# The first scan round's responses and state additions ahead of the placing of the choices, and the last block of the first expert layer ahead of the moments

## The chip, the cores and the metric

One NeuronCore of a Trainium2 chip runs the whole kernel in one launch. The metric is the device time in microseconds (us); lower is better. Three runs of the kernel before gave 1929.3, 1924.45 and 1923.44 us, so its median is 1924.45 us. The profile is of a fourth execution that took 1926.27 us.

## The reference, cut to what matters

The input is 8 sequences of 1024 tokens with 256 features. Two layers follow each other, each adding an attention-like part and a mixture of experts (MoE) to its input. Only the first layer is touched here:

```python
xn = _layernorm(x)
x = x + _L0_attn_ref(xn, ...) + _L0_ffn_ref(xn, ...)

# _L0_attn_ref: a linear state space scan of 16 states per feature, along the sequence
def step(h, x_t):
    h = jnp.einsum('dnm,bdm->bdn', A, h) + Bm[None] * x_t[..., None]
    y_t = jnp.einsum('dn,bdn->bd', Cm, h) + Dm * x_t
    return (h, y_t)
_, y = jax.lax.scan(step, h0, jnp.swapaxes(x, 0, 1))
y = gelu(_layernorm(y, ln_w, ln_b)) @ W_out.T + b_out      # then x + y

# _L0_ffn_ref: 8 experts, 2 chosen for each token, and a shared expert
topk_idx = jax.lax.top_k(masked, TOPK)[1]
y = jnp.einsum('tei,eih->teh', _silu(g) * u, w_down)       # the chosen experts' rows are summed by weight
```

The second layer normalizes this sum, takes one matrix product as its attention, and has an MoE of 8 experts with a fixed capacity.

## The kernel before, in words

The tokens lie as 64 tiles of 128 (`NT`), 8 tiles (`TPB`) to a sequence. The tile `y` holds them all, 128 x 64 x 256 in fp32; it is overwritten stage by stage. The line numbers are those of the kernel before.

**Stage 1, to about 205 us.** Each pair of tiles is normalized, turned, put through the router (L606) and the shared expert (L265, L280, L617). Every second sequence `route0` (L489) picks two experts for 16 tiles; the fourth `route0` ends this stage. Its steps are small VectorE instructions (L493 to L531, and L204 to L214 in the helper `pick_two`).

**The places (L662 to L723).** All choices of all tokens are counted, and each gets a place in a list sorted by expert, in blocks of 256 rows. Two matmuls count (L672, L676), ScalarE brings the counts from PSUM (L673, L677), and VectorE does the rest: L680 sums along the tokens, L684 to L697 find where each expert's blocks begin, L698 to L713 give each choice its place, L717 to L723 name the expert of each of the 71 blocks.

**The scan in 8 rounds.** The recurrence is worked out with matrix powers. A round `bt` takes 4 groups of 8 features. `krylov(bt)` (L292) makes the powers: `begin` (L301 to L314), then 7 levels k = 1, 2, 4 to 64; each level has for each of the 4 groups two matmuls into a PSUM tile `pk` (L324), then a VectorE copy (L331) and a ScalarE copy (L335, at the last level L333) out of it, on which the next level's matmuls of that group depend. There are two `pk` buffers. `rest(bt)` (L343) returns 16 steps that use the powers: `responses` (L348: matmuls L359, VectorE L368 and L369, and the DMA L372 of the responses to a DRAM scratch); four `adds` (L377: matmul L381, ScalarE copy L383, matmul L386, VectorE L390 of 0.6 us and L391 of 1.0 us); seven `chunk` (L398: matmuls L409, VectorE L413; the first is a copy, L402); four `outputs` (L417: the DMA L422 that loads the responses again, matmuls L433 and L438, and a copy of the round's features into `y`, L448 or L450).

**What is done between the steps.** The loop at L883 gives out, after each of a round's 16 steps, one step of `krylov(bt + 1)`, and a share of other work: in rounds 0 and 1 the `finds` (L730: VectorE L738, L741 and L745, ScalarE L749, matmul L751), which turn the places into lists of rows; in rounds 2 to 7 the 71 blocks of the first MoE. `block(n)` fetches the rows of block n + 1 (`bring`, L783: DMA L788 and gathers L791), finishes block n - 1 (`narrow`, L805: matmul L280, VectorE L810, scatter L813 into the DRAM tensor `yr`) and begins block n (`widen`, L801: L251, L255, L265, L270, L272, L273). The last block, number 70, is thus given out after the last step of the last round, and its own `narrow` follows it.

**The moments.** `first_moments` (L867) measures two sequences of the scan's finished output (16 pairs of L179 and L180 on VectorE), makes scales of them (L184 on ScalarE, L185 and L186 on VectorE) and normalizes the first sequence (8 times L191 on ScalarE). It is called after the last `outputs` and ahead of the last share of blocks.

**Stage 3, from about 782 us.** SyncE loads `base` and rows of `yr` (L955, L963), VectorE adds them (L976); meanwhile `flipped` (L923) turns and activates the normalized scan output (L932 on TensorE, L933 on ScalarE), `project` (L1003) multiplies by `W_out` (L1011) and adds (L1018); then moments again, and the second layer. From about 1000 us on the second MoE fills TensorE (L1415, L1433).

**What sets the order.** Each engine runs its own queue in order. The order in the queue is that of the source only roughly: a scheduler in the framework moves an instruction ahead of others where it expects it to be ready. In the kernel before it already draws the responses and additions of round 0 in among the instructions of the places, and the finds behind all levels of `krylov(1)`.

## Time and profile before

| what | value |
|---|---|
| median of three runs | 1924.45 us |
| the profiled execution, its time | 1926.27 us |
| its span in the trace | 1924.6 us (1.7 us lie around it) |
| mean granted TensorE clock | 0.969 |
| ScalarE, VectorE, GpSimd busy | 716.6 us (37%), 705.7 us (37%), 656.1 us (34%) |
| chain that ended last | TensorE 52% of the span, VectorE 3%, DMA 1%, ScalarE 1% |
| its largest lines | L1415 23%, L1433 23% (the second MoE), L1011 2% |
| first MoE's scatter, L813 | 142 times, 996 ns each |
| VectorE L179 (a tile's moments) | 128 times, median 397 ns |

How to read it: the trace gives the start of each instruction, its length, and, for a stretch in which the engine stood idle, what ended the wait. In the timeline a line has the start, the length, the engine, the line of the source with its operation, and in brackets the idle time before it with what ended it. PE is TensorE's matmuls, PEld its weight loads, DVE VectorE, ACT ScalarE, POOL GpSimd, SP SyncE; an engine's name with a q (SPq) is its queue, which issues DMAs. The granted clock is the share of TensorE's full clock that it was allowed. An fp32 matmul stands as two passes (x2).

### The profile page before, as it was taken

How to read it: one execution, taken by the hardware profiler on the slowest of the kernel's cores; microseconds unless marked ns; L12 is line 12 of the kernel's file. 1: busy time of each engine (PE TensorE's matmuls, PEld its weight loads, DVE VectorE, ACT ScalarE, POOL GpSimd, SP SyncE). 2: the span in 40 equal slices, each digit the busy share in tenths (PEclk: the TensorE clock that was granted, in tenths of full speed). 3: DMA queues.
4: the chain of work that ended last, by engine and by line, in shares of the span. 5: the costliest groups of instructions: out<-in, count | busy, mean ns of one | idle time of the engine just before them, and what ended most of it. 6: DMA issues, size and time to landing. Idle time of an engine off the chain costs nothing.

```text
span 1924.6 us, 24183 instructions
## 1 busy us (share of the span) xinstructions
PE 1790.2 (93%) x8619; PEld 1360.6 (71%) x8619; DVE 705.7 (37%) x2121; ACT 716.6 (37%) x1627; POOL 656.1 (34%) x668
## 2 busy tenths in 40 slices
PE   6987789999999999689959999999999999999996
PEld 5876667888888877579737667667666766766764
DVE  5854688444554444787751001101110110100110
ACT  6973354333333321679922222222222222222221
POOL 0000001666756766111023434343333333333322
PEclk9988899999999999889969999999999999999998
DMA  9565222565656666899533455443223232332211
GB/s 254 143 180 158 74 61 84 150 180 161 185 176 173 177 192 167 259 287 246 140 104 59 83 99 83 96 67 83 40 47 72 40 81 35 64 61 34 40 17 22
DMA packets 218520, 224.77 MB, mean 117 GB/s; under 512 B 50776, under 2 KB 190880, under 8 KB 218272
## 3 DMA queue, kind: packets, MB, share of 16 engines
q0 software_dynamic: 56928, 90.29, 23.7%
q1 hardware_dynamic: 158784, 130.54, 23.6%
q10 hardware_dynamic: 2688, 2.40, 0.4%
q8 instruction: 68, 1.11, 0.2%
q14 instruction: 52, 0.43, 0.1%
HBM read 136.87 MB, written 89.46 MB: 118 GB/s over the span
## 4 chain that ended last, share of the span: by engine, by line
PE 52%; DVE 3%; DMA 1%; ACT 1%; issue 1%; POOL 0%; POOLq 0%; SPq 0%; DVEq 0%; ACTq 0%
PE phe L1415 23%; PE poe L1433 23%; PE pd L1011 2%; PE px L1398 1%; PE pt L932 1%; PE pd L1076 1%; DMA xs<-yr 1%; DMA out_dram<-yo,invi 1%; DVE hl L1160 0%; DVE hh L1165 0%; ACT y L191 0%; PE pi L1175 0%; DVE st L179 0%; PE pt L1057 0%; DVE hb L976 0%
## 5 line engine op out<-in xcount | busy, mean ns | idle before, releaser
L1433 PE MATMUL poe<-w2t,hT 128*128 128x256 f32 x2048 | 447.3, 379 | 0.0
L1415 PE MATMUL phe<-xTe,w1t 128*128 128x512 f32 x1024 | 446.2, 594 | 0.6 <-DVE xTe L1399 0.6
L1433 PEld LDWEIGHTS poe<-w2t,hT 128*128 128x128 f32 x2048 | 386.7, 190 | 51.7 <-issue 0.5
L1415 PEld LDWEIGHTS phe<-xTe,w1t 128*128 128x128 f32 x1024 | 195.0, 191 | 233.1 <-issue 229.9
L1445 POOL DMA_INDIRECT out_dram<-yo,invi x128 | 201.8, 1577 | 446.0 <-DMA out_dram<-yo,invi 226.0
L1422 ACT ACTIVATE hT<-phe,b1T 128x512 f32<-128x512 f32 x256 | 176.0, 687 | 247.3 <-PE phe L1415 242.9
L1444 ACT ACTIVATE yo<-yo,gr 128x256 f32<-128x256 f32 x128 | 58.0, 500 | 441.4 <-DVE yo L1440 441.4
L1440 DVE TENSOR_TENSOR yo<-poe,b2t 128x512 f32<-128x512 f32 x64 | 44.3, 692 | 406.6 <-PE poe L1433 406.6
L1384 POOL DMA_INDIRECT xg<-xd,invi x128 | 124.6, 974 | 192.0 <-PE px L1398 86.2
L1399 DVE COPY xTe<-px 128x512 f32<-128x512 f32 x64 | 41.2, 686 | 382.6 <-PE px L1398 382.6
L813 POOL DMA_INDIRECT yr<-yo,goes x142 | 141.4, 996 | 65.3 <-DVE yo L810 27.8
L791 POOL DMA_INDIRECT xb<-xnd,choice x142 | 141.0, 993 | 46.9 <-issue 32.6
L324 PE MATMUL pk<-kr 128*128 128x129 f32 (+7 forms) x896 | 140.9, 296 | 9.4 <-ACT kr L335 8.6
L324 PEld LDWEIGHTS pk<-kr 128*128 128x128 f32 x896 | 124.7, 196 | 24.6 <-ACT kr L335 14.2
L265 PE MATMUL pgu<-xT,wb 128*128 128x256 f32 x568 | 138.8, 387 | 0.8 <-ACT xT L255 0.7
L786 POOL COPY wb<-wrow 1x1 int32<-1x1 int32 x71 | 12.8, 180 | 368.3 <-PE pgu L751 320.2
L265 PEld LDWEIGHTS pgu<-xT,wb 128*128 128x128 f32 x568 | 105.8, 192 | 26.8 <-ACT xT L255 12.6
L335 ACT COPY kr<-pk 128x256 f32<-128x256 f32 x192 | 69.6, 373 | 86.7 <-DVE kr L331 84.7
L270 ACT ACTIVATE sg<-pgu 128x256 f32<-128x256 f32 x87 | 33.4, 384 | 170.2 <-PE pgu L265 170.1
L272 DVE TENSOR_TENSOR hh<-pgu,sg 128x256 f32<-128x256 f32 x87 | 36.9, 424 | 127.3 <-ACT sg L270 127.1
L280 PE MATMUL pd<-wb,hh 128*128 128x256 f32 x284 | 77.1, 394 | 5.4 <-DVE hh L273 5.4
L810 DVE SCALAR_TENSOR_TENSOR yo<-pd,xb,bhalf 128x256 f32<-128x256 f32 x142 | 62.2, 479 | 49.0 <-PE pd L280 44.5
(323 smaller groups left out, 2349.6 us busy)
## 6 DMA issues: line engine op xcount, KB each, us to landing
wb<-wpk SPq DMA_DIRECT2D x71, 384.0 KB, 3.4
xnd<-xr SPq DMA_DIRECT2D x32, 512.0 KB, 8.5
hk<-kscr SPq DMA_DIRECT2D x32, 512.0 KB, 4.5
hb<-yr POOLq DMA_DIRECT2D x10, 1024.0 KB, 14.4
base<-y SPq DMA_DIRECT2D x8, 1024.0 KB, 4.4
hb<-base SPq DMA_DIRECT2D x8, 1024.0 KB, 10.2
out_dram<-y SPq DMA_DIRECT2D x8, 1024.0 KB, 14.2
xd<-xs SPq DMA_DIRECT2D x8, 1024.0 KB, 12.7
```

Source lines behind the costliest of these rows:

```text
L265: nc.tensor.matmul(pgu[:, j, :], lhsT=gu[:, j, c, :], rhs=xT[:, c, :], start=(c == 0), stop=(c == DC - 1),)
L280: nc.tensor.matmul(pd[:, q, :], lhsT=hh[:, q * P : (q + 1) * P], rhs=wb[:, 2 * DC * I : WW], start=True, stop=True,)
L324: nc.tensor.matmul(pk[:, j, :n], lhsT=t[:, 1 - j, P:], rhs=t[:, j, P - k : P - k + n], start=True, stop=True,)
L335: nc.scalar.copy(t[:, :, P:], pk[:, :, k : k + P])
L791: nc.gpsimd.indirect_dma_start(out=xb[:, q, : D + 1], out_offset=None, in_=xnd[:, :], in_offset=bass.IndirectOffsetOnAxis(ap=choice[:, 2 * ...
L810: nc.vector.scalar_tensor_tensor(yo[:, q, :], pd[:, q, :], xb[:, q, D : D + 1], bhalf, ALU.mult, ALU.add)
L813: nc.gpsimd.indirect_dma_start(out=next(yr_own)[:, :], out_offset=bass.IndirectOffsetOnAxis(ap=goes[:, 2 * n + q : 2 * n + q + 1], axis=0) ...
L1384: nc.gpsimd.indirect_dma_start(out=xg[:, q, :], out_offset=None, in_=xd[:, :], in_offset=bass.IndirectOffsetOnAxis(ap=invi[:, q0 + q : q0 ...
L1415: nc.tensor.matmul(ph, lhsT=w1t[:, c, h * P : (h + 1) * P], rhs=xT[:, c], start=(c == 0), stop=(c == DC - 1),)
L1422: nc.scalar.activation(hT[:, h], ph, AF.Relu, bias=b1T[:, e * HC + h : e * HC + h + 1])
L1433: nc.tensor.matmul(po[:, r, :], lhsT=hT[:, h, q + r, :], rhs=w2t[:, h, :], start=(h == 0), stop=(h == HC - 1),)
L1445: nc.gpsimd.indirect_dma_start(out=of[:, :], out_offset=bass.IndirectOffsetOnAxis(ap=invi[:, q0 + r : q0 + r + 1], axis=0), in_=yo[:, r, : ...
```

## The change

The change has two parts.

First, `rest` no longer takes the pool `toep` as an argument; it looks it up when `outputs` runs. So the steps of round 0 can be made before that pool exists, and their first five, `responses` and the four `adds`, are called right after the last `route0`, ahead of the source lines of the places. In the loop, round 0 skips these five; what is given out between the steps (powers of round 1, finds) is not changed.

Second, `first_moments` is called after the loop, so behind the last share of blocks, and its scales are made for each of the two sequences by themselves: two calls of L184, L185 and L186 on 8 columns in place of one on 16.

```diff
-        def rest(bt, toep):
+        pools = {}
+
+        def rest(bt):
...
-                hk = toep.tile([P, CH, P], F32, name="hk")
+                hk = pools["toep"].tile([P, CH, P], F32, name="hk")
...
-                hm = toep.tile([P, CH, NT], F32, name="hm")
+                hm = pools["toep"].tile([P, CH, NT], F32, name="hm")
...
                             route0(2 * TPB, slice((b - 1) * TPB, (b + 1) * TPB))
 
 
+            round0 = rest(0)
+            begun = 1 + GB
+            for step in round0[:begun]:
+                step()
+
+
             full = [P, NT, E]
...
         with tc.tile_pool(name="eb", bufs=3) as eb_, tc.tile_pool(name="toep", bufs=2) as toep:
+            pools["toep"] = toep
...
             def first_moments():
 
+
                 for b in range(2):
-                    moments(mo, first_mv[:, b], y[:, b * TPB : (b + 1) * TPB, :], TPB)
-                scales(first_mv, first_rstd, first_off)
-                ys = y[:, :TPB, :]
-                normalize_act(ys, ys, first_rstd[:, 0], first_off[:, 0], TPB)
+                    ys = y[:, b * TPB : (b + 1) * TPB, :]
+                    moments(mo, first_mv[:, b], ys, TPB)
+                    scales(first_mv[:, b], first_rstd[:, b], first_off[:, b])
+                    if b == 0:
+                        normalize_act(ys, ys, first_rstd[:, b], first_off[:, b], TPB)
...
             for bt in range(NBT):
-                steps = rest(bt, toep)
+                steps = rest(bt) if bt else round0
...
                 for s, step in enumerate(steps):
-                    step()
+                    if bt or s >= begun:
+                        step()
                     if s < len(ahead):
                         ahead[s]()
-                    if bt == NBT - 1 and s == len(steps) - 1:
-                        first_moments()
                     for f in part(s):
                         f()
+            first_moments()
```

Built, the two kernels have the same instructions but for one more L184, L185 and L186 each. The orders of SyncE's and GpSimd's queues are the same. The other three queues differ in two places only: from the end of the last `route0` to level 4 of `krylov(1)`, and from the second-last block's L810 to the first instructions of stage 3.

## The prediction

> **What bounds the kernel now.** I read the page first, its busy shares and slices. TensorE is busy 93% of the span, so what counts is where it is not.

> ```profile
> PE   6987789999999999689959999999999999999996
> ...
> PEclk9988899999999999889969999999999999999998
> ```

> A slice is 48.1 us. The fifth (192 to 241 us) and the seventeenth to nineteenth (770 to 914 us) have low digits, and the two edits lie there. Next, windows of 6 us and TensorE's timeline for the first place:

> ```profile
> 218.00:224.00 6.00, 0.04 (x2) 0.03 (x1) 6.00 (x15) 0.37 (x1) 0.00 (x0) 0.91 0.00 0
> 224.00:230.00 6.00, 4.05 (x16) 3.60 (x16) 3.26 (x16) 1.39 (x4) 0.00 (x0) 0.50 0.39 108
> 230.00:236.00 6.00, 5.72 (x29) 4.95 (x29) 1.28 (x7) 2.52 (x7) 0.00 (x0) 0.73 0.28 71
> ```

> ```profile
> 216.99 1.02 PE L386 MATMUL pm<-xc,vT 128*128 128x448 f32 x2 [0.18 <-ACT vT L383]
> 223.97 1.25 PE L324 MATMUL pk<-kr 128*128 128x132 f32 x4 [5.96 <-ACT kr L335]
> 227.17 15.42 PE L324 MATMUL pk<-kr 128*128 128x132 f32 x72 [1.95 <-ACT kr L335]
> 245.64 0.49 PE L751 MATMUL pgu<-wb,xb 128*128 128x284 bf16 x2 [3.05 <-ACT wb L749]
> ```

> In a window row the busy times are of PE, PEld, DVE, ACT and POOL, then comes the clock. From 212 to 224 us VectorE is full; TensorE stands still for 5.96 us, and its clock falls to 0.50 until about 233. From 227 us krylov(1) runs alone: matmuls, L331, L335, in a circle. The first find (L738) starts at 243.00, behind the last L331 in VectorE's queue.

> For the second place, the timeline from 764 to 782 us:

> ```profile
> 766.52 0.75 DVE L179 BATCH_NORM_STATS2 st<-y 128x6 f32<-128x256 f32 x2 [1.05 <-ACT y L450]
> ...
> 769.99 0.38 ACT L270 ACTIVATE sg<-pgu 128x256 f32<-128x256 f32 x1 [2.08 <-PE pgu L265]
> ...
> 772.76 0.46 DVE L810 SCALAR_TENSOR_TENSOR yo<-pd,xb,bhalf 128x256 f32<-128x256 f32 x1
> ...
> 773.59 0.42 DVE L272 TENSOR_TENSOR hh<-pgu,sg 128x256 f32<-128x256 f32 x1
> ...
> 774.71 2.08 PE L280 MATMUL pd<-wb,hh 128*128 128x256 f32 x4 [4.76 <-DVE hh L273]
> ...
> 777.09 0.86 DVE L810 SCALAR_TENSOR_TENSOR yo<-pd,xb,bhalf 128x256 f32<-128x256 f32 x2
> ...
> 781.86 0.38 SPq L955 DMA_DIRECT2D hb<-base  x1
> ```

> ```profile
> SPq L955 <- DMA yr<-yo,goes: 24.6, 1, 24.6
> ```

> The last line is from the waits (total, times, longest). L280 of block 69 was through at 766.79, yet L810 comes at 772.76: 16 pairs of L179 and L180, at 0.39 us each, stand before it. Block 70's L272 was ready at 770.37 and comes at 773.59. SyncE's L955, which opens stage 3, waits for the last scatter: the end of the last L810 sets it, 4.77 us after that starts (777.09 to 781.86).

> **Part one, the early steps.** The built VectorE queue holds the same instructions between the last pick and level 4; only their order changes. I walked through the new order with start distances of the timeline: a 128x512 step 0.60 us, L390 0.54, L391 0.88, L697 0.94, a 0.29 us step 0.33 if the next needs it and 0.20 if not, small ones 0.10.

> - L368 goes ahead of L511 at about 202.1 us. Its matmuls L359 (4 in 1.06 us) stand behind L280, which starts at 199.95, and end by 201.7: no wait. The first L390 waits some 0.3 us for L381, L383 and L386, and L617 0.1 us, as its L280 is now behind that L386. In exchange the 0.76 us that L617 waits now goes.
> - The four pairs L390, L391 (4 x 1.42 = 5.7 us) then fill the gaps of the pick. L520, which gives the counts' matmuls their input, comes at 212.0 instead of 207.76, L684 at 216.9 instead of 212.87. Behind it the pairs are missing, so the places catch up: L697 at 220.7 (218.92), the last L713 at 225.7 (226.31). The VectorE work of the stretch is the same, so its end stays within a microsecond.
> - In the place of the pairs stand L331 copies. Now only two of level 4's four are done by 226.7, the others come at 228.46 and 229.34, and level 8 begins at 230.45. Then all four are done by 226.5, limited at the end by the two pk buffers (matmuls 0.6, L331 0.2, L335 0.37 us), and level 8 begins at 227.1.
> - TensorE's longest gap becomes 1.8 us (215.6 to 217.4), not 5.96. At full clock four copies take 3.0 us (levels 16 and 32: 233.94 to 236.99), at half clock 3.5 (level 8: 230.45 to 233.94). At full clock L738 comes at 227.1 + 12.55 - 0.5 = 239.15: **3.85 us** earlier. At half clock each of level 4's last copies waits 0.9 us for the next, level 8 begins at 228.6, L738 comes at 241.15: 1.85 us. Below, nothing: if my walk is too short by 2 us; above, 4.5.

> I take 3.5, near the full clock, as a gap of 3.18 us (780.87 to 784.04) left it at 1.00. [...]

> Queues passed: L372 stays behind the last L535 in SyncE's queue, so it leaves at about 216 instead of 214.39; L422 waits for L713 as now (226.56), and its matmul L438 comes at 268.7, so nothing is late. The four L383 (0.27 us) go ahead of L313 on ScalarE, which stands idle 6.61 us in this stretch. GpSimd has nothing here. The finds and blocks behind keep their order, so they all start earlier by the same.

> **Part two, the moments.** In the new VectorE queue one L179 stands before block 69's L810, which starts at 766.9 (its L280 is through at 766.79) and ends at 767.8. Eleven halves of pairs follow, to 770.2; L272 starts at 770.4, as soon as L270 (769.99 + 0.38) is through; L273 at 771.2, L280 from 771.7 to 772.75 at the full clock's 1.03 us (TensorE idle 1.75 us, not 4.76). L810 starts at 772.8 in place of 777.09, and L955 4.77 later, at 777.6: **4.2 us** earlier. At half clock L280 takes 2.08 and it is 3.2.

> What is late next? ScalarE: L191 starts at 774.3 (now 775.76), 8 of them take 4.0, the second L184 0.31, so L933's table load starts at 778.6 (781.91) and L933 at 779.9 (783.21): 3.3 us earlier. Its L1011 begins at 781.7, but L1018 needs L976 first (790.71), which waits for DMAs issued behind L955. The DMA share is 0.9 to 1.1 from 783 to 812, all of it issued after L955, so it moves by 4.2 as a whole, and L976, L1018, the moments and L1029 (802.05) with it. The second L191s come wholly behind L933 (8, not 6: 1.0 us more); ScalarE waits 7.70 us before L1029, which covers it. The added L184, L185, L186 (0.31, 0.24, 0.16) lie in these waits. From 812 us on the order is the same, and the chain is mostly TensorE's; I take the shift whole to the end.

> **Sum.** -3.5 - 4.2 = -7.7. From the profiled execution's 1926.27 (1924.6 and 1.7 around it) this gives 1918.6; from the median, 1.8 lower, 1916.7. I say 1917.5.

> **Rivals.**
> 1. *The clock stays at half through level 8.* 1.85 + 4.2 = 6.1: 1919.1. For it: from 215.6 to 224.4 TensorE works only some 3 of 8.8 us, and at 247 the clock fell after 1 of 4.8. Against: the gaps there were longer (3.05).
> 2. *Only the moments count*, as VectorE ends the places about 3 us later than in my walk: 4.2, or 1921.0. For it: the walk rests on 0.1 us distances, some 80 of them.
> 3. *Only the early steps count*: stage 3 opens at 777.6, but L933 or the loads are held by something not seen before. 3.5: 1921.7. Against: L955 waits for the same scatters in both built queues, and 7 us lie between L1011 and L1018.
> 4. *Slower: the copies hold VectorE.* Ten L331 now stand among the places. If each waits for a matmul at half clock, 1.5 us as the longest such wait now, that is 15 us: 1917.5 + 15 = 1932.5. It decides against the change from 0.8 us each. For it: now each L331 in the place stretch finds its matmul long done. Against: at most three of the ten come less than 0.6 us after the copy that frees their buffer.
> 5. *No change*, the built orders being no measure of time: 1925.

> **How the numbers follow.** 0.3%, or 5.8 us, is about what a measurement of this kernel can tell from none: the bound is 1918.7. Forecast 0.55, rivals one 0.17, two 0.10, three 0.08, four 0.05, five 0.05. The range: 4.5 + 4.8 (no wait at all before the last L810) off the lowest run, 1923.44, gives 1914; only the half-clock 3.2, off the mean of median and profiled time, gives 1922. It leaves out rivals four and five and edges. Faster: 0.50 of the forecast, 0.08 of rival one, 0.04 of two and three, 0.62; slower 0.05; the rest, 0.33, within.

> **What would show it.** TensorE's clock at 224 to 230 us near 1 and no gap over 2 us from 215: else rival one. L331 of level 8 near 227 and L738 near 239: else two. Relative to L450's end: last L810 6.3 us after it (now 10.6), L955 11.1 (now 15.4), L976 from 20 (now 24.2): else three. Waits of L331 among the places over 0.8 us: four. I would be wrong wholly if stage 3's first loads waited for the moments instead of the last scatter.

## The result, and the profile after

| | before | after |
|---|---|---|
| median, runs | 1923.51 us, 22 runs (1920.95 to 1930.35) | 1918.81 us, 22 runs (1912.27 to 1926.0) |
| ratio, 95% interval | | 0.9975 [0.9965, 0.9984] |
| profiled execution, span | 1926.27, 1924.6 us | 1920.38, 1918.7 us |

The change makes the kernel faster by 0.25%, 4.7 us. The forecast was 1917.5 us (1914 to 1922) and its sum 7.7 off. So the time lies in the range, while the sum was too large by 3.0 us.

In the changed kernel the line numbers are higher: of those that count here L672, L676 (the counts' matmuls) are L680, L684; L520 is L522, L698 is L706, L713 is L721, L390 and L391 are L392 and L393, L386 is L388, L738 is L747, L450 is L452, L810 is L819, L955 is L966, L976 is L987, L1415 is L1426. L265 to L335 keep theirs.

The busy slices of the page of after, for TensorE and its clock:

```profile
PE   6987799999999998889869999999999999999996
...
PEclk9988899999999999889979999999999999999998
```

TensorE's fifth digit is 7 as before and the clock's is 8 as before: the first place is not visibly better. At the second place the seventeenth digit has gone from 6 to 8. Next the windows of after from 206 to 230 us (busy time of PE, PEld, DVE, ACT and POOL, then the clock), and TensorE's timeline there:

```profile
206.00:212.00 6.00, 4.53 (x12) 2.50 (x12) 4.40 (x18) 1.92 (x4) 0.00 (x0) 0.72 0.15 1
212.00:218.00 6.00, 3.75 (x16) 3.03 (x16) 5.91 (x24) 1.39 (x4) 0.00 (x0) 0.71 0.17 7
218.00:224.00 6.00, 4.53 (x18) 4.08 (x19) 4.31 (x23) 1.77 (x5) 0.00 (x0) 0.50 0.02 4
224.00:230.00 6.00, 5.42 (x32) 4.31 (x31) 1.51 (x9) 2.98 (x8) 0.00 (x0) 0.94 0.63 175
```

```profile
202.79 1.02 PE L388 MATMUL pm<-xc,vT 128*128 128x448 f32 x2
207.29 1.65 PE L680 MATMUL pm<-hot,before 128*128 128x512 f32 x2 [3.48 <-DVE kr L331]
208.73 1.91 PE L684 MATMUL pm<-hot,ones 128*128 128x512 f32 x2
...
213.81 3.75 PE L324 MATMUL pk<-kr 128*128 128x130 f32 x16 [1.99 <-ACT kr L335]
218.76 1.25 PE L324 MATMUL pk<-kr 128*128 128x132 f32 x4 [1.21 <-ACT kr L335]
```

The gap of 5.96 us is gone, but a new one of 3.48 us stands ahead of the counts' matmuls. The clock falls behind it: those matmuls take 1.65 and 1.91 us, where 1.10 and 1.02 were needed before, and from 216 to 224 us the clock is at 0.50. VectorE, whose queue has L706 next, waits for them, which it didn't before (L698). In the timelines of before:

```profile
208.20 1.10 PE L672 MATMUL pm<-hot,before 128*128 128x512 f32 x2
209.13 1.02 PE L676 MATMUL pm<-hot,ones 128*128 128x512 f32 x2
...
210.22 0.68 DVE L698 TENSOR_TENSOR hot<-hot,first 128x512 f32<-128x512 f32 x1
```

And in VectorE's of after, where it waits later for level 4's matmuls too:

```profile
210.68 0.69 DVE L706 TENSOR_TENSOR hot<-hot,first 128x512 f32<-128x512 f32 x1 [1.43 <-PE pm L684]
...
222.00 0.17 DVE L331 COPY kr<-pk 128x8 f32<-128x8 f32 x1 [0.47 <-PE pk L324]
...
222.88 0.17 DVE L331 COPY kr<-pk 128x8 f32<-128x8 f32 x1 [0.51 <-PE pk L324]
```

The second place, after's timeline from 759 to 772 us, and the wait ahead of stage 3:

```profile
759.36 0.59 ACT L452 COPY y<-py 128x512 f32<-128x512 f32 x1 [1.35 <-PE py L440]
...
759.98 0.43 DVE L179 BATCH_NORM_STATS2 st<-y 128x6 f32<-128x256 f32 x1 [1.05 <-ACT y L452]
...
760.32 0.86 DVE L819 SCALAR_TENSOR_TENSOR yo<-pd,xb,bhalf 128x256 f32<-128x256 f32 x2
...
763.86 0.42 DVE L272 TENSOR_TENSOR hh<-pgu,sg 128x256 f32<-128x256 f32 x1 [0.30 <-ACT sg L270]
...
765.06 1.13 PE L280 MATMUL pd<-wb,hh 128*128 128x256 f32 x4 [1.65 <-DVE hh L273]
...
766.23 0.88 DVE L819 SCALAR_TENSOR_TENSOR yo<-pd,xb,bhalf 128x256 f32<-128x256 f32 x2
...
771.38 0.38 SPq L966 DMA_DIRECT2D hb<-base  x1
```

```profile
SPq L966 <- DMA yr<-yo,goes: 20.7, 1, 20.7
```

One L179 stands ahead of block 69's L819 and L272 waits for ScalarE alone. L966 still waits for the last scatter, and comes 12.0 us behind the start of the last L452, in place of 15.9.

**Where the time went.** The two spans differ by 5.9 us, but that this is near the medians' 4.7 is chance: in 13 profiles the last scores of stage 1 (L653, in changed kernels L655 or L656, on ScalarE), which no edit touches, start anywhere from 188.5 to 198.4 us. So I cut each profile at events that both kernels have, in us. "scores to find" goes from the start of that last ScalarE instruction to the first find (L738, L747), "find to y" to the start of the last copy into `y` (L450, L452), "y to base" to SyncE's first base load (L955, L966), "base to MoE" to the second MoE's first matmul (L1415, L1426), and "MoE to end" to the end of the span.

| profile | scores to find | find to y | y to base | base to MoE | MoE to end |
|---|---|---|---|---|---|
| before | 44.7 | 522.9 | 15.9 | 216.5 | 926.2 |
| after | 43.5 | 522.8 | 12.0 | 219.8 | 927.5 |
| e1 early steps only | 43.9 | 521.0 | 15.9 | 217.3 | 927.3 |
| e2 moments only | 44.7 | 520.9 | 12.7 | 219.3 | 927.6 |
| e3 after, gap filled | 42.6 | 523.1 | 12.0 | 217.5 | 927.1 |
| e4 counts first | 41.3 | 520.8 | 12.0 | 217.2 | 927.1 |
| e5 before again | 44.7 | 597.5 | 15.9 | 218.7 | 927.3 |
| e6 after again | 43.5 | 604.3 | 12.3 | 217.8 | 926.9 |
| e7 scales undivided | 43.7 | 598.6 | 12.4 | 216.1 | 926.9 |
| e8 counts first, gap filled | 40.9 | 596.5 | 12.1 | 217.4 | 927.1 |
| e9 after, timed | 43.8 | 586.9 | 12.3 | 219.5 | 927.4 |
| e10 counts first, timed | 41.4 | 581.5 | 12.2 | 218.1 | 927.3 |
| e11 counts first, gap filled, timed | 41.0 | 578.4 | 12.1 | 217.9 | 927.2 |

Columns one and three hardly vary from execution to execution: a kernel's repeats agree within 0.5 us. They hold the effect: -1.2 and -3.9, together 5.1 us, against 4.7 measured. The chips of e5 to e8 and of e9 to e11 are other ones, with a longer stretch from find to y; there only comparisons within a chip count.

### The profile page after: what moved, and what is told of

Same layout as the page of the kernel before. It is cut to its first block, busy times and chain, and to the rows that moved or that the text cites. A ratio compares the mean times of both kernels' runs of the same rounds, so it can differ in the third digit from the quotient of the medians.

```text
span 1918.7 us, 24190 instructions
## 1 busy us (share of the span) xinstructions
PE 1794.2 (94%) x8619; PEld 1363.5 (71%) x8619; DVE 706.1 (37%) x2123; ACT 716.4 (37%) x1628; POOL 655.9 (34%) x668
## 4 chain that ended last, share of the span: by engine, by line
PE 58%; DVE 4%; DMA 2%; ACT 2%; issue 1%; POOL 0%; POOLq 0%; SPq 0%; DVEq 0%; ACTq 0%
PE phe L1426 23%; PE poe L1444 23%; PE pgu L265 2%; PE pd L1022 2%; PE px L1409 1%; PE pd L1087 1%; PE pt L943 1%; PE pd L280 1%; DMA xb<-xnd,choice 1%; PE py L440 1%; PE pk L324 1%; DMA out_dram<-yo,invi 1%; DVE st L179 1%; ACT hh L1184 0%; DVE hb L987 0%
## 5 line engine op out<-in xcount | busy, mean ns | idle before, releaser
L1426 PE MATMUL phe<-xTe,w1t 128*128 128x512 f32 x1024 | 447.2, 595 | 0.6 <-DVE xTe L1410 0.6
L1426 PEld LDWEIGHTS phe<-xTe,w1t 128*128 128x128 f32 x1024 | 195.4, 191 | 233.8 <-issue 230.6
L1410 DVE COPY xTe<-px 128x512 f32<-128x512 f32 x64 | 41.3, 687 | 383.7 <-PE px L1409 383.7
L822 POOL DMA_INDIRECT yr<-yo,goes x142 | 141.4, 996 | 60.1 <-DVE yo L819 31.8
L324 PE MATMUL pk<-kr 128*128 128x129 f32 (+7 forms) x896 | 140.8, 295 | 5.5 <-ACT kr L335 4.9
L265 PE MATMUL pgu<-xT,wb 128*128 128x256 f32 x568 | 140.3, 391 | 1.0 <-ACT xT L255 0.7
L324 PEld LDWEIGHTS pk<-kr 128*128 128x128 f32 x896 | 124.5, 196 | 21.2 <-ACT kr L335 10.1
L265 PEld LDWEIGHTS pgu<-xT,wb 128*128 128x128 f32 x568 | 106.4, 193 | 27.7 <-ACT xT L255 13.3
L335 ACT COPY kr<-pk 128x256 f32<-128x256 f32 x192 | 69.7, 373 | 85.2 <-DVE kr L331 82.6
L270 ACT ACTIVATE sg<-pgu 128x256 f32<-128x256 f32 x87 | 33.4, 384 | 171.1 <-PE pgu L265 171.0
L272 DVE TENSOR_TENSOR hh<-pgu,sg 128x256 f32<-128x256 f32 x87 | 36.9, 424 | 129.5 <-ACT sg L270 129.3
L819 DVE SCALAR_TENSOR_TENSOR yo<-pd,xb,bhalf 128x256 f32<-128x256 f32 x142 | 62.1, 479 | 48.2 <-PE pd L280 47.7
L280 PE MATMUL pd<-wb,hh 128*128 128x256 f32 x284 | 76.0, 389 | 2.1 <-DVE hh L273 2.0
## 6 DMA issues: line engine op xcount, KB each, us to landing
out_dram<-y SPq DMA_DIRECT2D x8, 1024.0 KB, 11.4
```

The costliest lines, as they stand in the source:

```text
L265: nc.tensor.matmul(pgu[:, j, :], lhsT=gu[:, j, c, :], rhs=xT[:, c, :], start=(c == 0), stop=(c == DC - 1),)
L280: nc.tensor.matmul(pd[:, q, :], lhsT=hh[:, q * P : (q + 1) * P], rhs=wb[:, 2 * DC * I : WW], start=True, stop=True,)
L324: nc.tensor.matmul(pk[:, j, :n], lhsT=t[:, 1 - j, P:], rhs=t[:, j, P - k : P - k + n], start=True, stop=True,)
L335: nc.scalar.copy(t[:, :, P:], pk[:, :, k : k + P])
L819: nc.vector.scalar_tensor_tensor(yo[:, q, :], pd[:, q, :], xb[:, q, D : D + 1], bhalf, ALU.mult, ALU.add)
L822: nc.gpsimd.indirect_dma_start(out=next(yr_own)[:, :], out_offset=bass.IndirectOffsetOnAxis(ap=goes[:, 2 * n + q : 2 * n + q + 1], axis=0) ...
```

## The experiments

**The two parts alone.** My theory at this point: the moments give 4 us, the early steps 1, since the new gap costs them the clock. The first kernel has only the early steps:

```diff
-            first_moments()
+                    if bt == NBT - 1 and s == len(steps) - 1:
+                        first_moments()
```

(with `first_moments` as before), the second has the early steps taken out:

```diff
-            for step in round0[:begun]:
-                step()
```

(and round 0 made in the loop again). Expected of them, on record:

> Only the early steps (responses and additions ahead of the places); the moments stay where they were before. Theory: the early steps are worth little, since TensorE now stands 3.5 us ahead of the counts' matmuls and runs them and krylov's next levels at half clock; last scores to first find 43.5 us (44.7 before, 43.5 after), first L450 on ScalarE to the first base load 16.0 as before, time about 1922.3 (1.2 off). Rival one, the sum on record: the early steps are worth 3.5 us and it is the gain of the moments that is lost: 1920.0, scores to find 41. Rival two, they are worth nothing but noise: 44.7 and 1923.5.

> Only the moments behind the last block; the early steps stay behind the places as before. Theory: the shorter way from the last outputs to the first base load (12.0 in place of 16.0 us) is kept to the end, and the 4 us by which the stretch from the roots to the mixture's first matmul was longer in the profile of after are that execution's own: time 1919.5, roots to the mixture about 196 to 198. Rival, the gain is given back in the third stage by the order itself: same 12.0 us, but roots to the mixture about 200, time 1922.5 to 1923.5.

Measured: early steps only 1922.87 us against 1923.46 of before on that chip, ratio 0.9989 [0.9976, 1.0002]; moments only 1921.16, 0.9982 [0.9967, 0.9997]. The times alone tell the parts from nothing barely or not at all; the stages tell them well. With the early steps alone, scores to find is 43.9 and y to base 15.9; with the moments alone 44.7 and 12.7. Each part moves its own stretch and leaves the other's as it was. The sum on record for part one (41) is out. The second expectation also asked for the time from the roots (the first L1029 of the next moments) to the second MoE's first matmul: 198.1 us with the moments alone, against 196.3 in before's and 200.3 in after's first profile. That is just above the theory's 196 to 198 and not the rival's 200; the time of the run lies between the two forecasts. In the profile of the early steps alone the same gap stands, with the same price:

```profile
211.88 1.87 PE L680 MATMUL pm<-hot,before 128*128 128x512 f32 x2 [3.50 <-DVE kr L331]
213.55 1.91 PE L684 MATMUL pm<-hot,ones 128*128 128x512 f32 x2
```

**The gap filled.** Into after's gap I put three products that nobody reads:

```diff
                 nc.scalar.copy(vT, pv[:, :P])
+                m["vT"] = vT
...
             for step in round0[:begun]:
                 step()
+            warm = ps_d.tile([P, 2, D], F32, name="pd").rearrange("p q d -> p (q d)")
+            for _ in range(3):
+                nc.tensor.matmul(
+                    warm[:, : CH * NS1], lhsT=m["vT"],
+                    rhs=xcols[:, (GB - 1) * CH : GB * CH, :NS1], start=True, stop=True,
+                )
```

> After, with three more products of the last addition's operands (L388's, 128x448, about 0.5 us each at full clock) into a bank that nobody reads, between the last addition's product and the counts' matmuls, so that TensorE stands still for under 2 us there. Theory, the clock is what part one lacks: the granted clock stays near 1 from 206 to 212 us and mostly to 224, the counts' matmuls take 0.9 us each in place of 1.65 and 1.91, last scores to first find falls from 43.5 to about 41.5 to 42.5, time 1917.5. Rival, VectorE's order is what it lacks: the clock rises but scores to find stays within 0.4 of 43.5, time 1918.8 as after. Third, 1.5 us of work are too little for the clock: it falls as in after, and the run tells nothing on the two.

Measured: 1919.56 us, 0.9981 [0.997, 0.9991]; scores to find 42.6. Its TensorE timeline, the first copy of level 8 in VectorE's, and windows:

```profile
204.00 2.42 PE L671 MATMUL pd<-xc,vT 128*128 128x448 f32 x6
207.65 1.10 PE L687 MATMUL pm<-hot,before 128*128 128x512 f32 x2 [1.24 <-DVE kr L331]
208.59 1.02 PE L691 MATMUL pm<-hot,ones 128*128 128x512 f32 x2
...
223.84 0.17 DVE L331 COPY kr<-pk 128x16 f32<-128x16 f32 x1 [0.74 <-PE pk L324]
```

```profile
210.00:214.00 4.00, 1.66 (x13) 1.27 (x11) 3.91 (x22) 1.10 (x4) 0.00 (x0) 1.00 0.54 12
214.00:218.00 4.00, 1.71 (x10) 1.33 (x11) 4.00 (x10) 0.89 (x3) 0.00 (x0) 1.00 0.00 0
218.00:222.00 4.00, 2.76 (x13) 2.42 (x13) 3.02 (x17) 1.02 (x3) 0.00 (x0) 0.56 0.03 6
222.00:226.00 4.00, 4.00 (x19) 3.67 (x19) 0.91 (x7) 1.57 (x5) 0.00 (x0) 0.59 0.70 186
```

(The products are 0.8 us each, not 0.5 as I wrote: the three stand as six passes, which took 2.42 us.) The clock stays at 1.00 until 218 us, the counts' matmuls take 1.10 and 1.02 again, and the wait of 1.43 us for them is gone from VectorE's timeline. The last place (L713 of before, L728 here) starts 28.6 us behind the last scores instead of 30.0. So the clock theory holds, for 0.9 of the 2.6 us by which part one stayed under its full-clock figure (3.85 less 1.2). The rest is not the clock at the counts. The clock still falls at 218 (0.56 from 218 to 222 us), while levels 2 and 4 give TensorE little to do (1.71 of 4 us from 214), and level 8 begins 30.4 us behind the scores; that these levels come so late because the counts stand behind the pairs is what the next kernel tries. The time of the run is no lower than after's, and 1917.5 was forecast; a microsecond can't be told from none here, only the stage shows it.

**The counts first.** If the pairs ought not to delay the step that feeds the counts, the steps can be given behind the counts' matmuls and still ahead of the places:

```diff
             round0 = rest(0)
             begun = 1 + GB
-            for step in round0[:begun]:
-                step()
...
             nc.scalar.copy(tot, pc.rearrange("p (i e) -> p e i", e=E))
+            for step in round0[:begun]:
+                step()
             cum = spare(4, [P, E, NT])
```

> After, but the responses and additions are given behind the two counts' matmuls and their copies, and still ahead of the places. In the built VectorE queue the step that feeds the counts (L520 of before) then comes ahead of the four pairs again, and the pairs stand among the first places. Theory: TensorE gets its counts' matmuls some 10 us after the last scores as before (14.2 in after), at full clock, and no gap over 3 us follows, so scores to find falls below after's 43.5, to about 42.5, time 1918. Rival: the pairs delay the copies of levels two and four as they did before, scores to find 44.7, time 1919.8, that is only the moments' gain.

Measured: 1917.52 us in 6 runs, 0.9967 [0.9952, 0.9983]; scores to find 41.3, better than the theory's 42.5. Its "no gap over 3 us" was wrong: TensorE stands still for 5.62 us later, and level 8 starts at half clock (0.50 from 224 to 228 us). Its timeline:

```profile
208.31 1.10 PE L678 MATMUL pm<-hot,before 128*128 128x512 f32 x2
...
217.57 0.84 PE L324 MATMUL pk<-kr 128*128 128x132 f32 x6
224.03 1.25 PE L324 MATMUL pk<-kr 128*128 128x132 f32 x4 [5.62 <-ACT kr L335]
```

What it gains beyond the filled gap's 42.6 is VectorE's order. In its timeline the first of level 4's copies (128x8) has gone ahead of the last two pairs, and the last starts at 225.5, 27.1 us behind the last scores (after: 30.9). Level 8's first copy (128x16) comes 28.8 us behind them, against 31.8 in after and 32.1 in before:

```profile
216.92 0.15 DVE L331 COPY kr<-pk 128x8 f32<-128x8 f32 x1
...
225.30 0.14 DVE L331 COPY kr<-pk 128x8 f32<-128x8 f32 x1
...
225.51 0.16 DVE L331 COPY kr<-pk 128x8 f32<-128x8 f32 x1
...
227.26 0.17 DVE L331 COPY kr<-pk 128x16 f32<-128x16 f32 x1
```

**Is something given back?** In the first profile of after, base to MoE is 3.3 us longer than in before's. Repeats of both tell whether the order does it; beside them the split of the scales, and a filled gap for the counts first.

> The kernel before once more, for its stage lengths. Theory: the stretch from the roots to the mixture's first matmul and the mixture itself, 196.2 and 926.3 us in its first profile against 200.3 and 927.5 in after's, are executions' own and lie near 198 and 927 here too; last scores to first find 44.7, last L450 to the first base load 16.0. Rival (the new order lengthens the third stage): 196.2 and 926.3 again, within 0.3.

> After once more. Theory: roots to the mixture about 198, as in the four runs so far, not 200.3; scores to find 43.5, last L452 to the first base load 12.0. Rival: roots to the mixture 200 again.

> After, with one undivided scales for both shifts as before, in place of one for each. Theory: the split is worth nothing, since the roots of before too lay in ScalarE's waits ahead of the loaded rows: last L452 to the first base load 12.0, base load to roots 19.5, time 1918.8. Rival: the split takes the first normalising off 8 pairs of moments, base load to the second round's start 1 to 3 us longer without it, time 1920 to 1922.

> The kernel with the counts first, and five more products of the last addition's operands (0.8 us each at full clock, into a bank that nobody reads) in the hole that TensorE has there, 5.62 us from 218.4 to 224.0. Theory: the clock no longer falls to 0.50 at 224 to 229, level 8 runs at full clock, last scores to first find falls from 41.4 to 40.5, time 1916.7. Rival: the chain of copies there is VectorE's, and the find comes at 41.4 as without them; worse, the products stand before level 4's and delay it, above 41.6.

These four ran on a chip on which before takes 1999.09 us. The two repeats are single runs (1998.9 and 2000.53 us), whose times decide nothing. Base to MoE: before 218.7, after 217.8, so the repeats turn the order round; roots to MoE: 197.9 and 198.3, the theory's 198. All kernels with the moments where they were: 216.5, 217.3, 218.7; moved, with divided scales: 217.2 to 219.8, mean 218.3. Most of the 3.3 is thus those executions' own; a loss of 0.8 us on average (218.3 less 217.5) is not excluded. The undivided scales give 1992.22 us, 0.9974 [0.9945, 1.0002], much the same y to base (12.4) and the shortest base to MoE of all (216.1): **the split is worth nothing that shows**, though the first L191 then starts 11.9 us behind the end of the last L452, in place of 7.6. (From the first base load to the roots it takes 21.3 us, where 19.5 was forecast; but 21.1 and 21.2 stand in two runs with divided scales, e2 and e9.) The five products put into the later gap of the counts first give 40.9 in place of 41.3 us (time 1992.01, 0.9973 [0.9948, 0.9997]); the truth lies between theory and rival, as TensorE still has gaps of 1.88 and 1.21 us behind them and the clock falls later (0.57 from 224 to 228 us):

```profile
214.96 3.92 PE L689 MATMUL pd<-xc,vT 128*128 128x448 f32 x10
218.72 0.84 PE L324 MATMUL pk<-kr 128*128 128x132 f32 x6
221.43 0.72 PE L324 MATMUL pk<-kr 128*128 128x132 f32 x4 [1.88 <-ACT kr L335]
223.36 1.31 PE L324 MATMUL pk<-kr 128*128 128x136 f32 x8 [1.21 <-ACT kr L335]
```

**The better version beside after.** Three kernels on one more chip, before at 1988.77 us:

> After once more, timed beside the next two on one chip. Theory: last scores to first find 43.5 us, last L452 to the first base load 12 to 12.7, base load to the mixture's first matmul between 216 and 220 as in all profiles of either order; 4.5 to 5 us off before, which is 1.2 of the early steps and 4 of the moments. Rival: the two gains don't add, 2 to 3 off.

> The counts ahead of the early steps, as the run of this name before. Theory: scores to find 41.4, so 2.1 under after on the same chip, 7 off before: the sum of the forecast, reached by another order. Rival: the two medians lie within 1 us of each other, and the stretch ahead of the finds is not what the end hangs on.

> The same with five products more in TensorE's hole. Theory: scores to find 40.9, as in its first profile, 0.5 under the kernel without them, less than these runs can tell apart; level 8's first L331 28.3 us behind the last scores (28.9 without them). Rival: its 40.9 was that execution's own: 41.4 again.

Measured: after 1986.64, 0.9986 [0.996, 1.0012]; counts first 1979.97, 0.9955 [0.9929, 0.9982]; with the products 1980.79, 0.9967 [0.9943, 0.9991]. All three stage lengths repeat: 43.8, 41.4, 41.0. On this chip the times spread over 20 us, so after can't be told from before in them; its 2.1 us off would fit the rival too. The counts first is clear of before on both chips, with the lowest median on both. Its median lies 6.7 us under after's here and 1.3 on the first chip; the stage itself is shorter by 2.4 and 2.1 us. The rest of the 6.7 stays open; from find to y, which the order doesn't touch, these two profiles differ by 5.4.

## Why the prediction came out as it did

- **What bounds the place of the early steps.** Right in kind: the first find hangs on level 8, and that on VectorE. The walk gave the step that feeds the counts (L520) 13.7 us behind the last scores; 13.74 was measured. It fails at the next one.
- **The step that failed: "TensorE's longest gap becomes 1.8 us (215.6 to 217.4), not 5.96".** I looked for gaps behind the counts only, and not ahead of them, where VectorE's 4 us of delay of L520 leaves TensorE without work: 3.48 us. At half clock the counts' matmuls hold VectorE for 1.43 us, which now has no pair to fill the time; the step L684 of before comes 20.2 us behind the scores, not 18.6, the last place 30.0, not 27.4, level 8 31.8, not 28.8. **Part one gave 1.2 us, the term had 3.5.** Filling that gap gave 0.9 back. The gaps of 3.48 and 3.50 us had counts' matmuls of 1.65 to 1.91 us behind them, the one of 1.24 us had 1.10 and 1.02. But it doesn't take so long a gap: in after's profile the clock fell again at 214.52 us, with no gap over 1.99 us in the 3.41 us before, of which TensorE was busy for 1.42 (last section).
- **A second step failed, and it weighs more: "I take 3.5, near the full clock".** With the gap filled, level 8 still comes 30.4 us behind the scores and the find 42.6; rival one had 30.3 and 42.85 (228.6 and 241.15 less 198.3), the full clock 28.8 and 40.85. So 1.7 of the missing 2.6 us stand without the gap, and there rival one is right to 0.3 us. Its sign came true as well: at the place that lay from 224 to 230 us before, 5.2 us earlier in after's profile, the clock was at 0.50. In absolute times, as the prediction gave its signs, after would have passed (clock 0.94 from 224 to 230, no gap over 2 us from 215). I asked how long the longest gap was; rival one asked how little TensorE had to do (3 of 8.8 us), and that was the better question. The gap of 3.18 us that I leaned on left TensorE busy for 1.54 us of 779.32 to 782.73 and for 2.10 us of 782.73 to 786.14 in before's profile, 0.45 and 0.62 of the time. That the clock alone makes these 1.7 us is not shown, since no run has this order at full clock through level 4.
- **Part one's size was to be had, by another order.** 40.85 us from the scores to the find was the walk's figure at full clock; the counts first has 41.3, the same with products 40.9.
- **Part two.** Right step by step. From the end of the last L452: last L819 6.3 us (forecast 6.3), L966 11.4 (11.1), L987 20.2 (20). It gave 3.9 in after, 3.2 in the run with the moments alone and 3.6 to 3.9 in the other runs, for a term of 4.2. Its alternative at half clock, 3.2, is what L280's 1.13 us speak against (2.08 in before's profile).
- **Carried whole to the end.** Not refuted and not shown to a microsecond: base to MoE varies by 2 to 3 us for either order.
- **Rivals.** Two (only the moments count, 4.2) is nearest to the measured 4.7; yet its mechanism, a walk that is 3 us short, is half right: the last place is 2.6 us later than walked, 1.4 of them by the clock at the counts (30.0 less the 28.6 with the gap filled). Four, the copies that hold VectorE, is out in its size: among the places only two L331 wait for a matmul, 0.47 and 0.51 us, not 15 in all. But this 1.0 us stands with the gap filled too, and with the 1.4 it is nearly all of what the last place lost. Three and five are out by the stage lengths.
- **What was luck.** The sum was 3.0 us too large, yet 1917.5 is only 1.3 from the measured 1918.81: it was taken off some 1925.2, and 22 runs put the kernel before at 1923.51, 1.7 lower. The range held since its upper edge had only part two at half clock and nothing of part one; 0.62 for faster by over 0.3% was too much for an effect of 0.25%.

## What to carry to other kernels

When independent work is moved ahead to fill gaps of one engine, ask which engine waits for the step that is now behind it, ahead of that step as well as behind it: here the pairs filled VectorE's gaps and opened one in TensorE, and two thirds of that part's gain went, 0.9 us of it through the clock at the next matmuls. Give such work behind the step that another engine needs, and ahead of the one that only the same engine needs. And compare single profiles by stages between events that both kernels have, never by their spans: ten microseconds of untouched code lay between executions here.
